# Four two-pass row tiles and six pairs, weight sums one at a time, and the pairs' products in the transposes' banks

## The chip, the cores and the metric

The kernel runs on one core of a Trainium2 chip. The metric is the device time of one execution in microseconds (us). The engines of the core work side by side, each through its own queue of instructions in order: PE (TensorE, matrix products; its weight loads are listed apart as PEld), DVE (VectorE), ACT (ScalarE), POOL (GpSimd), and SP (SyncE), which issues most of the DMAs. Products of PE go to PSUM, a memory of eight banks, and DVE or ACT take them out from there; a bank can be written again only when it has been read.

## The reference

Input x has 2048 rows of 1024 numbers (4 x 512 x 1024), all float32. Two layers follow each other, each with a residual and a layer norm:

```
attn = (w1 @ w2.T) * sparse_mask
x = layernorm(x + gelu(x @ attn + b2))
w_l, w_h = dequant(qweight, lut4, 4 bits), dequant(qweight, lut8, 8 bits)
y = where(norm(x) > 64, x @ w_h.T, x @ w_l.T) + bias
out = layernorm(x + y)
```

The mask is nonzero only in a band around the diagonal. A dequantised weight is a table entry, chosen per output row by the bits of the code, which lie in bit planes.

## The kernel before

**Tiles and stages.** The 2048 rows are 16 row tiles of 128. Weights, both as products' operands, stay in the core's memory. A first stage builds `attn` for the band and dequantises the left half of the 4-bit weight (output columns 0 to 511). The right half is dequantised in eight more steps of the generator `low` (`steps(1)`), woven into the second stage; each step is three or four predicated copies on DVE with table lines made by ACT and POOL. A finished block of the weight is transposed into `wT` by PE (`transpose_pending`), and the identity is added to the weight, so that a product already holds the residual.

**Attention tile** (`attention(n, xT)`): PE multiplies the transposed tile by the band (L467) into an accumulator `mm`, DVE adds b2 and writes `z` (L482), ACT does the gelu (L483), DVE adds x (L485), ACT sums squares (L354), POOL makes the factor (L356, L357), DVE normalises (L361).

**Two-pass tile**: `ffn_half(n, xT, h)` multiplies the transposed tile by one half of `wT` (eight matmuls 512 wide, L495, each two records in the trace), and `combine` (L507) takes the product out of `mm`. ("left", n) is h = 0, ("right", n) is h = 1; after the right one `finish_rows` normalises the row tile (the same chain of DVE, ACT, POOL and DVE) and stores it. The tile's transposed x is made once by PE, with copies out of PSUM on ACT (L263, L264), and kept under the tag `early{n}`.

**Pair** (`ffn_pair`): two row tiles are taken together as a 2 x 2 block product by the Strassen-Winograd scheme: seven products of four matmuls each instead of eight. It needs sums of weight blocks, t1 to t4 (`weight_sums`, L544 to L547, DVE), and of input blocks, s1 to s4 (`pair_inputs`: a copy of the first on ACT, s1 and s3 on DVE, a copy of a22 on ACT, s2 and s4 on POOL). Its input is transposed without PE: `squares` transposes 32 x 32 squares on DVE (L554), writes them to DRAM (L558) and reads them back in four DMAs per tile (L564, `rows`). Products go to banks u (two buffers), v and w of the pool `ps_pair`. `prepare_pair(n, part)` does one third of the preparation of the pair that starts at tile n; within a pair the next one is prepared (`between`).

**Order.** The list `todo` is the order of work of the second stage: attention of tiles 0 to 3, then lefts with attention between, two more attention tiles (8 and 9), then rights, each followed by one of the attention tiles 10 to 15. The transposes of the next entry of the list are issued ahead of the present one. At ("right", 0) all dequantisation is finished, the pool of the dequantisation is closed, the pool `last` is opened in its place, and tiles 12 to 15 of x (from `SOON` on) are loaded into it. `check_outside` reads the parts of the mask outside the band and sums their absolute values, one block at a time after a left or an attention tile. Instructions are scheduled by the program's framework in the order of the program where their dependences allow it; each engine then has a fixed list.

**PSUM.** `ps_tr` (four banks, transposes) lives to the end; `ps_mm` (two accumulators of two banks, taken in turn by attention tiles and halves) is closed before the pairs, and `ps_pair` takes its four banks. The buffer tag `z` (two buffers) is shared by z, the normalised output `o` and the mask blocks `raw`.

```
todo = [("attention", n) for n in range(4)]
for m in range(EARLY):
    todo.append(("left", m))
    if m < 4:
        todo.append(("attention", 4 + m))
todo += [("attention", 8), ("attention", 9)]
for m in range(EARLY):
    todo += [("right", m), ("attention", 10 + m)]
```

Of the kernel before, what the change touches and what calls it, by code (L numbers as in the profile page):

```python
# [9 lines left out]
FP = mybir.dt.float32  # L10
# [19 lines left out]
WIN = P + 2 * BAND  # L30
SQ = 32
Q = P // SQ
EARLY = 6
AHEAD = 2


# [156 lines left out]
def kernel(  # L193
# [13 lines left out]
    nc = tc.nc  # L207
# [6 lines left out]

    with ExitStack() as main:
        const = main.enter_context(tc.tile_pool(name="const", bufs=1))
        ps_tr = main.enter_context(tc.tile_pool(name="ps_tr", bufs=4, space=bass.MemoryType.PSUM))
        first_ps, first_sb = main.enter_context(ExitStack()), main.enter_context(ExitStack())
        ps_mm = first_ps.enter_context(
            tc.tile_pool(name="ps_mm", bufs=2, space=bass.MemoryType.PSUM)  # L220
        )
        band = main.enter_context(tc.tile_pool(name="band", bufs=1, side="right"))
        dq = first_sb.enter_context(tc.tile_pool(name="dq", bufs=1, side="right"))
# [302 lines left out]
        def ffn_half(n, xT, h):  # L526
            ps = ps_mm.tile([P, D], FP, tag="mm", name="mm")
            product(ps[:, :HALF], xT, h)
            combine(n, h, ps[:, :HALF], bias_bc[:, ts(h, HALF)])
            if h == 1:  # L530
                finish_rows(n)

# [4 lines left out]
        b11, b12 = wT[:, :KH, :HALF], wT[:, :KH, HALF:]  # L537
        b21, b22 = wT[:, KH:, :HALF], wT[:, KH:, HALF:]

        def weight_sums(pool):  # L540
            t1, t2, t3, t4 = (
                pool.tile([P, KH, HALF], FP, tag=f"t{i}", name=f"t{i}") for i in range(1, 5)
            )
            nc.vector.tensor_tensor(t1, b12, b11, ALU.subtract)  # L544
            nc.vector.tensor_tensor(t2, b22, t1, ALU.subtract)
            nc.vector.tensor_tensor(t3, b22, b12, ALU.subtract)
            nc.vector.tensor_tensor(t4, b21, t2, ALU.subtract)  # L547
            return t1, t2, t3, t4

        def squares(pool, n):  # L550

# [39 lines left out]
            nc.gpsimd.tensor_tensor(s4, a12, s2, ALU.subtract)  # L591
            return a11, a12, a22, s1, s2, s3, s4

        def ffn_pair(pool, n, blocks, weights, between):

            a11, a12, a22, s1, s2, s3, s4 = blocks
            t1, t2, t3, t4 = weights
# [35 lines left out]
        def count_odd():  # L633


            nc.vector.tensor_scalar(ssq, ssq, EST_T * EST_T, None, ALU.is_gt)
            nc.vector.tensor_scalar(outside, outside, 0.0, None, ALU.is_equal)
            nc.vector.tensor_scalar(outside, outside, -1.0, 1.0, ALU.mult, ALU.add)
            n_odd = const.tile([P, 1], FP, name="n_odd")
            nc.vector.tensor_reduce(n_odd, odd, AX.X, ALU.add)  # L640
            pc = ps_tr.tile([P, 1], FP, tag="tr", name="pc")
            nc.tensor.matmul(out=pc[0:1, :], lhsT=n_odd, rhs=ones, start=True, stop=True)
            nc.vector.tensor_copy(count, pc[0:1, :])

        todo = [("attention", n) for n in range(4)]
        for m in range(EARLY):
            todo.append(("left", m))
            if m < 4:  # L650
                todo.append(("attention", 4 + m))
        todo += [("attention", 8), ("attention", 9)]
        for m in range(EARLY):
            todo += [("right", m), ("attention", 10 + m)]
        unpack_after = [("attention", 1), ("left", 0), ("attention", 4), ("left", 1)]
        unpack_after += [("attention", 6), ("left", 2), ("left", 3), ("left", 4)]

        kept = {}
        rows, blocks = {}, {}
# [17 lines left out]
        ready = prepare(*todo[0])  # L677
        checks = 0
        for i, (what, n) in enumerate(todo):
            if (what, n) == ("right", 0):  # L680
                steps(100)
                transpose_pending(0)
                first_sb.close()
                last = main.enter_context(tc.tile_pool(name="last", bufs=1, side="right"))
                for m in range(SOON, NT):
                    load_x(last, m)
            if (what, n) == ("left", 0):
                transpose_pending(0)
            xT = ready
            if i + 1 < len(todo):  # L690
                ready = prepare(*todo[i + 1])
            if what == "attention":
                attention(n, xT)
                if n > 8 and checks < KT:
                    check_outside(checks)
                    checks += 1
            else:
                ffn_half(n, xT, 0 if what == "left" else 1)
                if what == "left" and n > 1:
                    check_outside(checks)  # L700
                    checks += 1
                if (what, n) == ("right", 0):
                    weights = weight_sums(last)
            if (what, n) in unpack_after:
                steps(1)
            if what == "right" and n >= EARLY - 3:
                prepare_pair(EARLY, n - (EARLY - 3))
        while checks < KT:
            check_outside(checks)
            checks += 1  # L710
# [4 lines left out]
        for n in range(EARLY, NT, PAIR):  # L715

            def between(part, done, m=n + PAIR):
                with tc.issue_after(done.ins):
                    prepare_pair(m, part)

            ffn_pair(ps_pair, n, blocks[n], weights, between)
            if n == EARLY:
                count_odd()

# [41 lines left out]
```

## Time and profile before

| | |
|---|---|
| median of 3 runs | 381.35 us (381.2 to 381.87) |
| the profiled execution | 380.86 us |
| its span (first to last instruction) | 379.1 us |
| first stage | 0 to 60.8 us |
| attention tiles, lefts, dequantisation | 60.8 to 172.1 us |
| rights with attention tiles | 172.1 to 245.6 us |
| five pairs | 245.6 to 368.4 us |
| last normalisation and store | 368.4 to 379.1 us |

Durations used for the change, means of one instruction from the groups: a product matmul record 0.602 us (L495; records overlap, and they follow each other every 0.43 us), squares on DVE 2.02 us (L554), a weight sum 2.29 us (L544 to L547), z 1.22 us (L482), gelu 1.05 us (L483), the add of x 1.28 us (L485), the sum of squares 1.15 us (L354), a normalisation 0.81 us (L361), a combine 0.68 us (L507). One instruction's record overlaps the next by up to 0.08 us on DVE, so that they follow each other a little faster than these.

How to read it: "the clock" is the share of TensorE's full speed that was granted. An engine's idle time is named by what ended it. A busy engine counts only where the end of the kernel hangs on it; so stages are looked at one by one.

### The profile page before, as it was taken

Reading aid. Unit: us, or ns where it says so; the run is one execution under the profiler, and the core shown is the slowest. Engines: PE = TensorE matmul, PEld = TensorE weight load, DVE = VectorE, ACT = ScalarE, POOL = GpSimd, SP = SyncE. Lnnn points to the kernel's source line nnn. Section 1 sums busy time; section 2 is a strip of 40 time slices with the busy share of each in tenths; the row PEclk is TensorE's granted clock in tenths of the full one; section 3 lists DMA queues with packets and bytes.
Section 4 is the critical chain, followed back from the end, with each engine's and each line's share of the span. In section 5 each row is a group of like instructions: output and inputs, shape, how many; then the busy total and the mean of one; then the engine's idle time right before and its main releaser. Section 6 shows DMA issues by size and latency. Waiting matters only on the chain.

```text
span 379.1 us, 3687 instructions
## 1 busy us (share of the span) xinstructions
PE 336.0 (89%) x1226; PEld 206.7 (55%) x1226; DVE 231.2 (61%) x344; ACT 149.2 (39%) x228; POOL 119.9 (32%) x144
## 2 busy tenths in 40 slices
PE   3599785989989898988999999599999999999980
PEld 3588574975666464583666656344444444444430
DVE  2599798889968895059744536453482563825221
ACT  0952843986485465244355443311111302113011
POOL 1990881866265511003022212210130400304000
PEclk9699996989999999998999999889999999999996
DMA  9998104900010111019242211107126162461102
GB/s 225 356 353 269 76 3 163 390 2 0 0 45 3 41 42 43 0 62 311 72 139 96 102 55 55 51 10 217 47 119 166 55 231 47 165 167 55 55 3 118
DMA packets 26906, 41.80 MB, mean 110 GB/s; under 512 B 7424, under 2 KB 19456, under 8 KB 26880
## 3 DMA queue, kind: packets, MB, share of 16 engines
q1 hardware_dynamic: 21616, 40.90, 31.6%
q10 hardware_dynamic: 5264, 0.59, 1.1%
q8 instruction: 11, 0.18, 0.2%
q14 instruction: 15, 0.12, 0.1%
HBM read 27.85 MB, written 13.63 MB: 109 GB/s over the span
## 4 chain that ended last, share of the span: by engine, by line
PE 42%; DVE 26%; POOL 12%; ACT 9%; issue 8%; DMA 1%; ACTq 0%; POOLq 0%; DVEq 0%
PE u L604 18%; PE w L604 9%; ACT junk L354 5%; PE mm L467 5%; PE v L604 5%; POOL root L307 4%; PE mm L495 4%; DVE root L312 3%; DVE x L485 3%; DVE root L311 3%; POOL r L357 3%; DVE z L482 3%; POOL e L307 2%; DVE e L310 2%; DVE root L316 2%
## 5 line engine op out<-in xcount | busy, mean ns | idle before, releaser
L495 PE MATMUL mm<-wT,xT 128*128 128x512 f32 x192 | 86.2, 602 | 5.4 <-DVE x L507 2.7
L356 POOL TENSOR_SCALAR r<-ss 128x1 f32<-128x1 f32 x32 | 10.4, 325 | 200.0 <-ACT junk L354 199.8
L354 ACT ACTIVATE junk<-x,nm 128x1024 bf16<-128x1024 f32 x32 | 36.8, 1149 | 82.9 <-DVE nm L351 82.7
L467 PE MATMUL mm<-attn,xT 128*128 128x198 f32 (+2 forms) x320 | 63.9, 358 | 5.3 <-ACT xT L264 5.3
L467 PEld LDWEIGHTS mm<-attn,xT 128*128 128x128 f32 x320 | 56.1, 201 | 13.7 <-ACT xT L264 5.7
L495 PEld LDWEIGHTS mm<-wT,xT 128*128 128x128 f32 x192 | 36.1, 193 | 47.2 <-issue 40.5
L303 ACT ACTIVATE e<-v,lt,diff 128x1024 f32<-128x1024 uint8 x32 | 38.2, 1240 | 11.4 <-DVE v L278 9.7
L307 POOL TENSOR_SCALAR root<-v,diff,lt 128x1024 f32<-128x1024 uint8 x16 | 36.4, 2277 | 8.2 <-DVE root L316 7.4
L307 POOL TENSOR_SCALAR e<-v,diff,lt 128x1024 f32<-128x1024 uint8 x16 | 29.6, 1852 | 28.5 <-DVE v L278 25.5
L604 PE MATMUL u<-t,halves 128*128 128x512 f32 x80 | 36.0, 592 | 0.0
L361 DVE TENSOR_SCALAR o<-x,nm,r 128x1024 f32<-128x1024 f32 x16 | 13.0, 812 | 34.4 <-POOL r L357 34.4
L421 PE MATMUL mm<-w2T,w_sb 128*128 128x268 f32 (+1 forms) x128 | 30.1, 390 | 4.1 <-issue 2.3
L264 ACT COPY xT<-pt 128x512 f32<-128x512 f32 x44 | 23.4, 583 | 23.4 <-PE pt L263 18.3
L483 ACT ACTIVATE z<-z 128x1024 f32<-128x1024 f32 x16 | 16.9, 1054 | 31.0 <-DVE z L482 31.0
L421 PEld LDWEIGHTS mm<-w2T,w_sb 128*128 128x128 f32 x128 | 24.3, 200 | 8.1 <-issue 2.5
L311 DVE COPY_PREDICATED root<-v,e 128x1024 f32<-128x1024 uint8 x16 | 22.9, 1433 | 7.8 <-POOL root L307 7.8
L310 DVE COPY_PREDICATED e<-v,e 128x1024 f32<-128x1024 uint8 x16 | 24.3, 1524 | 3.4 <-ACT e L303 3.4
L263 PE MATMUL pt<-ident,x 128*128 128x128 f32 x176 | 23.0, 275 | 3.6 <-DVE x L361 1.8
L485 DVE SCALAR_TENSOR_TENSOR x<-z,x 128x1024 f32<-128x1024 f32 x16 | 20.4, 1276 | 9.2 <-ACT z L483 9.2
L604 PEld LDWEIGHTS u<-t,halves 128*128 128x128 f32 x80 | 15.2, 190 | 19.1 <-issue 18.9
L586 ACT COPY halves<-rows 128x1024 f32<-128x1024 f32 x5 | 5.2, 1042 | 51.2 <-DMA rows<-there 39.0
L361 DVE TENSOR_SCALAR x<-x,nm,r 128x1024 f32<-128x1024 f32 x16 | 13.0, 810 | 19.3 <-POOL r L357 19.3
(74 smaller groups left out, 425.3 us busy)
## 6 DMA issues: line engine op xcount, KB each, us to landing
x<-in_L_attn_x_dram SPq DMA_DIRECT2D x16, 512.0 KB, 6.9
out_dram<-o SPq DMA_DIRECT2D x16, 512.0 KB, 2.6
there<-squares SPq DMA_DIRECT2D x10, 512.0 KB, 3.0
rows<-there SPq DMA_DIRECT2D x40, 128.0 KB, 3.4
w_raw<-in_L_attn_w_dram SPq DMA_DIRECT2D x8, 512.0 KB, 5.6
w_sb<-in_L_attn_w_dram SPq DMA_DIRECT2D x3, 1024.0 KB, 7.8
w_sb<-in_L_attn_w_dram SPq DMA_DIRECT2D x2, 512.0 KB, 5.1
raw<-_L_attn_sparse_mask_dram SPq DMA_DIRECT2D x2, 413.0 KB, 2.9
```

Source lines behind the costliest of these rows:

```text
L264: nc.scalar.copy(dst[:, g * (HALF // P) : (g + 1) * (HALF // P), :], pt)
L303: nc.scalar.activation(entry[j], plane(0), AF.Identity, scale=d_k, bias=l_k)
L307: nc.gpsimd.tensor_scalar(entry[j], plane(0), d_k, l_k, ALU.mult, ALU.add)
L310: nc.vector.copy_predicated(entry[2], plane(1), entry[3])
L311: nc.vector.copy_predicated(root, plane(1), entry[1])
L354: nc.scalar.activation(junk, u, AF.Square, bias=nm, accum_out=ss)
L361: nc.vector.tensor_scalar(dst, u, nm, r, ALU.add, ALU.mult)
L421: nc.tensor.matmul(out=ps[:, : hi - lo], lhsT=w1_sb[s][:, k, :], rhs=w2T[:, k, lo:hi], start=(k == 0), stop=(k == KT - 1),)
L467: nc.tensor.matmul(out=ps[:, a:b], lhsT=xT[:, s, :], rhs=attn[:, s, a - lo : b - lo], start=h not in fresh, stop=hi == D or (h == 0 and wi ...
L485: nc.vector.scalar_tensor_tensor(xt, z, 1.0, xt, ALU.mult, ALU.add, accum_out=total)
L495: nc.tensor.matmul(out=ps, lhsT=xT[:, k, :], rhs=wT[:, k, ts(h, HALF)], start=(k == 0), stop=(k == KT - 1),)
L604: nc.tensor.matmul(out=ps, lhsT=a[:, k, :], rhs=b[:, k, :], start=start and k == 0, stop=stop and k == KH - 1, skip_group_check=True,)
```

## The change

EARLY goes from 6 to 4: tiles 0 to 3 are two-pass tiles, tiles 4 to 15 make six pairs. The order of work follows: after the four lefts, attention tiles 8 to 11 come ahead of the rights (before: 8 and 9), and the four rights are followed by attention tiles 12 to 15. The places of the dequantisation steps in this order move up by at most one entry or two. The dequantisation is closed, `last` opened and x of tiles 12 to 15 loaded at ("attention", 10), two attention tiles ahead of the first right. The four weight sums are no longer made together at the first right: t1 is issued after the combine of right 0, t2 after that of right 1 and so on, each held back until that combine (`tc.issue_after`). The first pair's preparation comes after rights 1, 2 and 3, after the weight sum (before: after rights 3, 4 and 5). In PSUM the two pools change places: `ps_mm` lives to the end and `ps_tr` is closed before the pairs, so that the pairs' banks u, v and w are those of the transposes; the one small product of `count_odd` goes to `ps_mm`.

```
-EARLY = 6
+EARLY = 4
...
-        ps_tr = main.enter_context(tc.tile_pool(name="ps_tr", bufs=4, space=bass.MemoryType.PSUM))
+        ps_mm = main.enter_context(tc.tile_pool(name="ps_mm", bufs=2, space=bass.MemoryType.PSUM))
         first_ps, first_sb = main.enter_context(ExitStack()), main.enter_context(ExitStack())
-        ps_mm = first_ps.enter_context(
-            tc.tile_pool(name="ps_mm", bufs=2, space=bass.MemoryType.PSUM)
+        ps_tr = first_ps.enter_context(
+            tc.tile_pool(name="ps_tr", bufs=4, space=bass.MemoryType.PSUM)
         )
...
-            combine(n, h, ps[:, :HALF], bias_bc[:, ts(h, HALF)])
+            done = combine(n, h, ps[:, :HALF], bias_bc[:, ts(h, HALF)])
             if h == 1:
                 finish_rows(n)
+            return done
...
+        sums_of = {1: (b12, b11), 2: (b22, 1), 3: (b22, b12), 4: (b21, 2)}
+        weights = {}
+
+        def weight_sum(pool, i):
+
+            plus, minus = sums_of[i]
+            weights[i] = pool.tile([P, KH, HALF], FP, tag=f"t{i}", name=f"t{i}")
+            minus = weights[minus] if isinstance(minus, int) else minus
+            nc.vector.tensor_tensor(weights[i], plus, minus, ALU.subtract)
...
         for m in range(EARLY):
-            todo.append(("left", m))
-            if m < 4:
-                todo.append(("attention", 4 + m))
-        todo += [("attention", 8), ("attention", 9)]
+            todo += [("left", m), ("attention", 4 + m)]
+        todo += [("attention", n) for n in range(4 + EARLY, SOON)]
         for m in range(EARLY):
-            todo += [("right", m), ("attention", 10 + m)]
+            todo += [("right", m), ("attention", SOON + m)]
         unpack_after = [("attention", 1), ("left", 0), ("attention", 4), ("left", 1)]
-        unpack_after += [("attention", 6), ("left", 2), ("left", 3), ("left", 4)]
+        unpack_after += [("attention", 5), ("left", 2), ("attention", 6), ("left", 3)]
...
-            if (what, n) == ("right", 0):
+            if (what, n) == ("attention", SOON - 2):
                 steps(100)
                 transpose_pending(0)
                 first_sb.close()
...
-                if (what, n) == ("right", 0):
-                    weights = weight_sums(last)
+                if what == "right":
+                    with tc.issue_after(done.ins):
+                        weight_sum(last, n + 1)
+                        if n >= EARLY - 3:
+                            prepare_pair(EARLY, n - (EARLY - 3))
             if (what, n) in unpack_after:
                 steps(1)
-            if what == "right" and n >= EARLY - 3:
-                prepare_pair(EARLY, n - (EARLY - 3))
```

In the changed kernel the lines from L540 on move by one or two (the products of a pair, L604 before, are L605).

More of the change, by code (lines that the diff above doesn't have):

```diff
@@ L538 @@
         b21, b22 = wT[:, KH:, :HALF], wT[:, KH:, HALF:]
[L540 to L548, printed above, removed]
+        sums_of = {1: (b12, b11), 2: (b22, 1), 3: (b22, b12), 4: (b21, 2)}
[5 more added lines that the diff above has]
+            nc.vector.tensor_tensor(weights[i], plus, minus, ALU.subtract)
         def squares(pool, n):
@@ L592, in pair_inputs, with ffn_pair @@
             return a11, a12, a22, s1, s2, s3, s4
-        def ffn_pair(pool, n, blocks, weights, between):
+        def ffn_pair(pool, n, blocks, between):
             a11, a12, a22, s1, s2, s3, s4 = blocks
-            t1, t2, t3, t4 = weights
+            t1, t2, t3, t4 = (weights[i] for i in range(1, 5))
             u = pool.tile([P, HALF], FP, tag="u", name="u", bufs=2)
@@ L640, in count_odd @@
             nc.vector.tensor_reduce(n_odd, odd, AX.X, ALU.add)
-            pc = ps_tr.tile([P, 1], FP, tag="tr", name="pc")
-            nc.tensor.matmul(out=pc[0:1, :], lhsT=n_odd, rhs=ones, start=True, stop=True)
-            nc.vector.tensor_copy(count, pc[0:1, :])
+            pc = ps_mm.tile([P, D], FP, tag="mm", name="pc")
+            nc.tensor.matmul(out=pc[0:1, 0:1], lhsT=n_odd, rhs=ones, start=True, stop=True)
+            nc.vector.tensor_copy(count, pc[0:1, 0:1])
         todo = [("attention", n) for n in range(4)]
         for m in range(EARLY):
-            todo.append(("left", m))
-            if m < 4:
-                todo.append(("attention", 4 + m))
-        todo += [("attention", 8), ("attention", 9)]
+            todo += [("left", m), ("attention", 4 + m)]
+        todo += [("attention", n) for n in range(4 + EARLY, SOON)]
         for m in range(EARLY):
-            todo += [("right", m), ("attention", 10 + m)]
+            todo += [("right", m), ("attention", SOON + m)]
         unpack_after = [("attention", 1), ("left", 0), ("attention", 4), ("left", 1)]
-        unpack_after += [("attention", 6), ("left", 2), ("left", 3), ("left", 4)]
+        unpack_after += [("attention", 5), ("left", 2), ("attention", 6), ("left", 3)]
         kept = {}
@@ L697 @@
             else:
-                ffn_half(n, xT, 0 if what == "left" else 1)
+                done = ffn_half(n, xT, 0 if what == "left" else 1)
                 if what == "left" and n > 1:
@@ L719, in between @@
                     prepare_pair(m, part)
-            ffn_pair(ps_pair, n, blocks[n], weights, between)
+            ffn_pair(ps_pair, n, blocks[n], between)
             if n == EARLY:
```

## The prediction, made before the changed kernel had run

> **What bounds the kernel now.** I read the busy shares first, then busy time by stage, then who TensorE waited for, then the chain of work that ended last. TensorE (PE) is busy 89% of the span:
>
> ```profile
> PE 336.0 (89%) x1226; PEld 206.7 (55%) x1226; DVE 231.2 (61%) x344; ACT 149.2 (39%) x228; POOL 119.9 (32%) x144
> ```
>
> By stage (start:end, length, then busy time of PE, its weight loads, DVE, ACT, POOL, then granted clock, DMA share, GB/s): attention tiles with left halves, the last attention tiles before the right halves, right halves with attention, the five pairs.
>
> ```profile
> 60.80:163.00 102.20, 94.60 (x419) 66.79 (x420) 75.48 (x103) 61.76 (x95) 45.20 (x48) 0.96 0.18 68
> 163.00:187.00 24.00, 21.46 (x96) 14.88 (x95) 20.03 (x20) 10.49 (x19) 3.66 (x8) 0.93 0.54 175
> 187.00:245.60 58.60, 53.97 (x209) 34.06 (x207) 29.08 (x56) 26.29 (x48) 14.32 (x34) 0.98 0.20 75
> 245.60:365.20 119.60, 119.60 (x275) 52.80 (x276) 56.99 (x99) 18.41 (x27) 18.51 (x28) 0.98 0.34 109
> ```
>
> The pair stage is pure PE. In the others PE is nearly full, so its work counts one for one and its few waits count besides. The waits of PE from 60 to 260 us (waited for: total, times, longest):
>
> ```profile
> PE mm L467 <- ACT xT L264: 5.3, 2, 4.7
> PE u L604 <- DVE z L482: 4.6, 1, 4.6
> PE mm L495 <- DVE x L507: 2.7, 2, 1.4
> PE mm L495 <- ACT wT L264: 2.5, 1, 2.5
> ```
>
> The 4.6 is the first pair waiting for the last attention tile's z; the 2.5 is the first right half waiting for the last weight transposes. The chain shows why z is late (start, length, what; one right half with its attention tile):
>
> ```profile
> 205.61 0.69 DVE x L507 x2
> 206.31 0.60 DVE halves L587
> 207.28 1.25 ACT junk L354 x2
> 209.53 0.67 issue
> 210.20 1.23 DVE z L482
> 211.45 1.07 ACT z L483
> 212.54 1.24 DVE x L485 x2
> 214.07 1.25 ACT junk L354 x2
> 215.67 0.56 POOL r L357
> 216.26 0.81 DVE x L361
> 217.37 0.61 DVE x L507 x2
> ```
>
> From one combine (L507) to the next is 11.76 us, 11.1 without the 0.60 for halves. PE needs 6.87 (16 records of a half) + 3.60 (attention) + 0.87 (transposes) = 11.34 for the same iteration. So the in-order DVE queue is as long as PE's work, with about 0.2 us to spare.
>
> **What the Trainium skill says.** "TensorE: Matmul & The Clock Gate", Part 1: after an idle window of some 3.4 us PE runs at half rate for about as long. The trace agrees: after the 4.63 us wait the first eight records took 5.76 us to the next product instead of 3.43, so the wait cost 2.3 more; after 2.54 us before the first right half, 1.5 more (8.38 instead of 6.87 to the next work). The same page (Architectural detail) has ACT and DVE as strict FIFO queues, which the chain above shows. "DMA: Bandwidth & Descriptors" (Anatomy of one DMA) gives a DMA about 2 us fixed whatever its size; here squares to DRAM land in 3.0 us and rows in 3.4 (medians), so the round trip is more than two such.
>
> **The change, part by part.**
>
> (1) PE work. Tiles 4 and 5 lose two passes each (4 x 6.87) and two sets of transposes (2 x 0.87): -29.2. The sixth pair adds 7 products x 3.43 = +24.0. Net -5.2.
>
> (2) Up to the end of left half 3 (135.5 us before) nothing changes: the order of DVE is the same up to there, PE only gets one weight transpose earlier. DVE is what bounds here: z of attention 6 came at 134.26, 10 us after its products, and the last dequantisation ended at 140.5. Moving two copy-predicated instructions ahead of z delays attention 7 by nothing I can price (z at about 136.8, PE there at 137.3). The next attention tile takes the accumulator of left 3, whose combine comes behind the same dequantisation at 142.4: I keep a 1.3 us wait.
>
> (3) From 135.5 to the first right half, PE: five attention tiles 18.0, five sets of x transposes 4.35, three of weights 2.6, the wait 1.3: 26.3, so the first right half starts at 161.8 instead of 172.1. The weight transposes sit two attention tiles ahead of it, so the 2.5 wait and its slow restart of 1.5 go. Covered by: ACT copies the last wT at about 156. In return x12 to x15 are loaded after these transposes, just ahead of their use: SP issues them at about 153, the first x load of four landed 3.7 us after its issue (3.7/5.8/7.8 least, median, most), and PE reaches x12's transposes after 0.87 + 3.60 = 4.5. I take 0; if x12 came last of four, 3.3 and a restart. The mask checks are queued behind these loads on SP; their ACT instructions wait for them with the second half of x12's transposes behind, needed only 7 us later.
>
> (4) Right halves with attention 12 to 15, PE: 4 x 6.87 + 4 x 3.60 + 3 x 0.87 = 44.5. Here DVE gets new work: one weight sum of 2.2 us after each combine, a stream transpose of 1.95 after the second and third, none of which had a place in this chain before (the four sums and both transposes ran at 168 to 186, while right half 0 and one attention tile kept PE busy). The queue of the changed kernel, with the lengths of the chain above (combine 0.69, statistics 2.35 from nm to the normalisation, z 1.2, gelu 1.1, x 1.3): first iteration 13.1, second 12.1, third 12.2, against 11.34 for PE. z of attention 11 is also late, so the first combine starts 1.8 after its product. With R the end of right half 0 (168.7): combines start at R+1.8, +14.9, +27.0. Attention 14 reuses the accumulator of attention 13, whose z ends at R+24.6, where PE is ready at R+22.7: 1.9 lost. Attention 15 waits for z of 14 (R+36.8; ready at R+36.0): 0.8. Bounds: nothing, if the two accumulators absorb it; 6, if each stop also restarts slowly. I take 2.7 and 0.5 for one partial restart.
>
> (5) Start of the pairs. Their four banks are now those of the transposes, free once ACT has copied the last xT, long before: the 4.6 wait and the 2.3 restart go. Late next is s1 of tiles 4 and 5: the stream transpose of tile 5 ends at R+34.7, DRAM and back 3.2 + 1.7 of issues + 3.0 gives rows at R+42.6, s1 at R+43.3 to 44; PE wants it one product after its start, at R+43.9. Behind that waiting instruction on DVE stand the last normalisation, s3, the first add of the pair, z and x of attention 15 and two more stream transposes, on POOL s2; on SP the rows are behind one store, on ACT the copy of a22 holds gelu of 15. Adds must free u and w within 6.87 us: the second is 0.4 late. I take 0.6; between 0 and 4.
>
> (6) Pairs: six of 24.03 = 144.2, +0.3 as the five showed (122.8 = 120.2 + 2.3 + 0.3). After the last product 10.7 us as before (368.4 to 379.1).
>
> Sum: 161.8 + 44.5 + 3.2 + 0.6 + 144.5 + 10.7 = 365.3 us of span, 13.8 less. The profiled execution took 380.86 for a span of 379.1, that is 1.8 around it: 367.1. The median of the runs, 381.35, is 0.5 higher than the profiled one, half of which I add: 367.3.
>
> **The rivals.**
>
> A: DVE keeps up and neither stop happens: 3.8 less, 363.5. For it: durations on DVE overlap by some 0.08 us each, and two accumulators allow a lag of several us. Against it: the chain of before left only 0.2 us and it gets 2.2 to 4.2 more per iteration.
>
> B: the x loads come late. All four share 16 DMA engines, and a mask check before them in SP's queue waits for a buffer. PE then idles 3.3 before attention 11 and restarts slowly (2.3): 367.3 + 5.6 = 372.9. For it: in the trace these loads and the squares kept the DMA engines over 90% busy for 10 us. Against: no squares go out at that time now, and x12 is first in the queue.
>
> C, slower than before: the added DVE work, with rows arriving late, stops PE in each right-half iteration long enough to halve the clock. One such stop costs its idle plus 2.3 us; to lose the 14 us gained it takes four of 3.5 + 2.3 = 23.2 in place of my 3.8, so 367.3 + 19.4 = 386.7. It decides once an iteration of the queue passes about 11.34 + 3.6 = 15 us (4 x 3.6 = 14.4 more). For it: written with nothing overlapped, an iteration of that queue is 15.4. Against: the new order puts combine and nm of the next tile between the waits, which brings it to 12.2.
>
> Not a rival with its own time but part of (2): if dequantisation is late, removed left halves only turn into waits; that costs up to 3.
>
> **How the numbers follow.** Forecast 0.60, A 0.18, B 0.15, C 0.04, anything else 0.03 (two thirds of it faster). The range takes in A with 1 us of margin and B: 362.5 to 372.9. 0.2% (0.8 us) is what a measurement can tell from no change: faster 0.95, same 0.01, slower 0.04.
>
> **What would show it.** Right: no wait of the first u product for z; first right half near 162 with no wait for wT; 6 x 24 us of pairs; short waits of the attention products (L467) for z in the right-half stage, 2 to 4 us in all. Wrong: a DMA wait at the transposes of x12 (B); PE below full clock between 170 and 210, or the w product waiting for halves (C); PE full in that stage (A).

## The result, and the profile after

The changed kernel takes 376.09 us (median of 4 runs, 375.64 to 376.31) against 381.61 us for the kernel before beside it (4 runs, 381.2 to 382.13): a ratio of 0.9853, 95% interval 0.9836 to 0.987. It is faster, by 5.5 us instead of the 14 forecast, and lies 3.2 us above the top of the range.

The profiled execution took 375.64 us for a span of 373.9. The page's busy times and shares of the span:

```profile
PE 327.9 (88%) x1202; PEld 199.9 (53%) x1202; DVE 238.4 (64%) x351; ACT 147.9 (40%) x226; POOL 125.0 (33%) x146
```

PE is busy 8.1 us less than before (the work taken away is 5.2, and two products that ran slowly after waits are gone besides), and the span is only 5.2 shorter: waits have come in. The stages of the changed kernel, in the columns of the table of stages before (attention tiles ahead of the rights, rights with attention, first pair and the door of the second, the other pairs):

```profile
135.60:164.50 28.90, 26.06 (x166) 23.35 (x165) 18.98 (x28) 18.96 (x36) 5.91 (x16) 1.00 0.28 100
164.50:212.20 47.70, 44.95 (x170) 27.74 (x169) 30.33 (x46) 22.25 (x44) 8.12 (x22) 1.00 0.34 110
212.20:242.00 29.80, 26.16 (x62) 10.70 (x61) 19.12 (x31) 8.36 (x14) 7.89 (x14) 1.00 0.31 90
242.00:362.00 120.00, 119.10 (x278) 52.54 (x277) 58.26 (x103) 18.62 (x28) 21.05 (x29) 1.00 0.36 114
```

PE idles 2.8 us in each of the first two and 3.6 in the third, and 0.9 in the last, where the pairs of before, once begun, had no idle time at all. The granted clock is 1.00 in all of them, so none of this is a slow restart. PE's waits of the changed kernel from 60 to 260 us (total, times, longest):

```profile
PE mm L467 <- ACT xT L264: 5.7, 3, 4.7
PE pt L263 <- ACT wT L264: 3.6, 3, 1.7
PE u L605 <- DVE x L618: 2.9, 2, 2.0
PE mm L467 <- DVE z L482: 2.8, 2, 1.9
...
PE w L605 <- DVE nm L351: 1.2, 1, 1.2
PE w L605 <- DVE halves L588: 0.4, 1, 0.4
```

The wait of the first u product for z (4.6) is gone, and so is that of the first right half for wT (2.5). New are the waits for z (L482) in the rights' stage, and those of products u and w in the first two pairs for additions on DVE (L618, and L620 behind the small nm L351) and for s1 (L588). The chain of work of one right half with its attention tile, in the changed kernel (start, length, what):

```profile
185.82 0.61 DVE x L507 x2
186.43 2.21 DVE t L549
...
188.71 1.94 DVE squares L555
...
190.80 1.25 ACT junk L354 x2
...
192.40 0.56 POOL r L357
...
193.71 1.23 DVE z L482
194.96 1.07 ACT z L483
196.05 1.25 DVE x L485 x2
```

Between combine and z stand now a weight sum and a stream transpose, 4.15 us of work that was not there before. The combines start at 172.76, 185.74, 197.39 and 210.73, 12.7 apart in the mean; PE needs 11.34 for each iteration. PE had finished right 3 at 206.65, so DVE comes to the pairs 4.1 us behind. In the kernel before it was 2.9 (right 5 ended at 237.37, its combine began at 240.22), so not all of this is new. What DVE does at the door of the pairs is seen in the timelines of the changed kernel's first pair. First PE (start, length, operation; in brackets the idle time before and what ended it):

```profile
212.21 3.60 PE L605 MATMUL u<-wT,halves 128*128 128x512 f32 x8
216.24 3.70 PE L605 MATMUL w<-t,halves 128*128 128x512 f32 x8 [0.44 <-DVE halves L588]
221.94 3.67 PE L605 MATMUL u<-t,halves 128*128 128x512 f32 x8 [2.00 <-DVE x L618]
226.81 3.67 PE L605 MATMUL w<-wT,halves 128*128 128x512 f32 x8 [1.20 <-DVE nm L351]
```

The third product is added onto the first in the bank u, so it waits until the addition L618 has read the first out; the fourth waits in the same way for the addition on w (L620). DVE in the same stretch:

```profile
210.73 0.69 DVE L507 SCALAR_TENSOR_TENSOR x<-mm,bias_bc 128x512 f32<-128x512 f32 x1
...
211.41 2.28 DVE L549 TENSOR_TENSOR t<-wT,t 128x2048 f32<-128x2048 f32 x1
...
215.50 0.69 DVE L588 TENSOR_TENSOR halves<-rows 128x512 f32<-128x512 f32 x1
217.78 1.75 DVE L361 TENSOR_SCALAR o<-x,nm,r 128x1024 f32<-128x1024 f32 x1 [1.59 <-POOL r L357]
219.45 1.74 DVE L589 TENSOR_TENSOR halves<-rows 128x512 f32<-128x512 f32 x1
221.12 0.68 DVE L618 TENSOR_TENSOR x<-u,bias_bc 128x512 f32<-128x512 f32 x1
```

And POOL:

```profile
217.71 1.27 POOL L591 TENSOR_TENSOR halves<-halves 128x512 f32<-128x512 f32 x1
219.05 1.59 POOL L592 TENSOR_TENSOR halves<-halves 128x512 f32<-128x512 f32 x1
```

The addition (L618) could have run at 215.8, when its product was done, but stands behind o, which waits for right 3's statistics, and behind s3. Both took a microsecond longer than the 0.81 and 0.69 us that they take elsewhere, exactly while POOL made s2 and s4.

### The profile page after: what moved, and what is told of

It is laid out like the page before. It is cut to its first block, busy times and chain, and to the rows that moved or that the text cites. A ratio compares the mean times of both kernels' runs of the same rounds, so it can differ in the third digit from the quotient of the medians.

```text
span 373.9 us, 3676 instructions
## 1 busy us (share of the span) xinstructions
PE 327.9 (88%) x1202; PEld 199.9 (53%) x1202; DVE 238.4 (64%) x351; ACT 147.9 (40%) x226; POOL 125.0 (33%) x146
## 4 chain that ended last, share of the span: by engine, by line
PE 35%; DVE 25%; POOL 17%; ACT 12%; issue 8%; DMA 1%; ACTq 0%; POOLq 0%; DVEq 0%
PE u L605 18%; PE w L605 9%; POOL root L307 7%; PE v L605 6%; ACT junk L354 5%; POOL e L307 4%; DVE x L485 4%; DVE root L312 3%; POOL r L357 3%; DVE z L482 2%; DVE root L316 2%; ACT z L483 2%; PE mm L467 2%; DVE t L549 2%; DVE e L310 2%
## 5 line engine op out<-in xcount | busy, mean ns | idle before, releaser
L467 PE MATMUL mm<-attn,xT 128*128 128x198 f32 (+2 forms) x320 | 62.9, 353 | 8.5 <-ACT xT L264 5.7
L467 PEld LDWEIGHTS mm<-attn,xT 128*128 128x128 f32 x320 | 54.4, 196 | 16.9 <-ACT xT L264 6.5
L495 PE MATMUL mm<-wT,xT 128*128 128x512 f32 x128 | 56.5, 594 | 1.6 <-DVE x L507 1.6
L605 PE MATMUL u<-t,halves 128*128 128x512 f32 x96 | 43.4, 595 | 2.9 <-DVE x L618 2.9
L307 POOL TENSOR_SCALAR root<-v,diff,lt 128x1024 f32<-128x1024 uint8 x16 | 38.9, 2433 | 8.1 <-DVE root L316 7.4
L495 PEld LDWEIGHTS mm<-wT,xT 128*128 128x128 f32 x128 | 23.7, 190 | 28.9 <-issue 26.3
L605 PEld LDWEIGHTS u<-t,halves 128*128 128x128 f32 x96 | 18.0, 190 | 26.8 <-issue 25.8
L587 ACT COPY halves<-rows 128x1024 f32<-128x1024 f32 x6 | 6.3, 1047 | 58.4 <-DMA rows<-there 46.5
L311 DVE COPY_PREDICATED root<-v,e 128x1024 f32<-128x1024 uint8 x16 | 22.7, 1416 | 8.8 <-POOL root L307 8.8
L264 ACT COPY xT<-pt 128x512 f32<-128x512 f32 x40 | 21.4, 587 | 10.2 <-DVE attn L428 5.1
L312 DVE COPY_PREDICATED root<-v,e 128x1024 f32<-128x1024 uint8 x16 | 24.7, 1547 | 0.1
```

The source lines that it names most:

```text
L307: nc.gpsimd.tensor_scalar(entry[j], plane(0), d_k, l_k, ALU.mult, ALU.add)
L311: nc.vector.copy_predicated(root, plane(1), entry[1])
L312: nc.vector.copy_predicated(root, plane(2), entry[2])
L467: nc.tensor.matmul(out=ps[:, a:b], lhsT=xT[:, s, :], rhs=attn[:, s, a - lo : b - lo], start=h not in fresh, stop=hi == D or (h == 0 and wi ...
L495: nc.tensor.matmul(out=ps, lhsT=xT[:, k, :], rhs=wT[:, k, ts(h, HALF)], start=(k == 0), stop=(k == KT - 1),)
L605: nc.tensor.matmul(out=ps, lhsT=a[:, k, :], rhs=b[:, k, :], start=start and k == 0, stop=stop and k == KH - 1, skip_group_check=True,)
```

## The experiments

The question is where 8.6 us of the forecast went: the span is 373.9 and not 365.3. The theory: DVE's in-order queue, which carries the sums and the transposes of the first pair through the rights' stage, arrives late at the pairs, and hands its lateness to PE as waits for the additions. Rivals: the rows of the first pair come late by DMA; the earlier dequantisation steps cost the time before right 0; the buffers of z are held by the mask checks; the banks alone did it all.

Each kernel was timed beside the kernel before; times are medians, ratios are to the kernel before with their 95% intervals.

**The kernel before with the two pools exchanged, and nothing else.** EARLY stays 6.

```
-        ps_tr = main.enter_context(tc.tile_pool(name="ps_tr", bufs=4, ...))
+        ps_mm = main.enter_context(tc.tile_pool(name="ps_mm", bufs=2, ...))
...
-        ps_mm = first_ps.enter_context(tc.tile_pool(name="ps_mm", bufs=2, ...))
+        ps_tr = first_ps.enter_context(tc.tile_pool(name="ps_tr", bufs=4, ...))
```

> The kernel before with nothing but the banks swapped (six two-pass tiles, five pairs, sums together). The wait of 4.6 us for z and the slow restart of 2.3 go, and no new wait comes, since s1 and s3 are ready early there: theory 1 and my reckoning of the banks: 374 to 376. Rival (the first adds of the pair then wait behind the last attention tile's work on DVE, as in the changed kernel): 377 to 380.

376.03 us, ratio 0.9866 (0.985 to 0.9883): as fast as the whole change, within the intervals. The first product u starts at 240.18 instead of 245.60. PE's waits in the pairs of this kernel:

```profile
PE u L604 <- DVE nm L351: 1.7, 1, 1.7
PE w L604 <- DVE x L619: 0.6, 1, 0.6
```

The 4.6 us wait for z and its restart are gone, and 2.3 us of waits for additions have come, the same kind as in the changed kernel but smaller; s1 and s3 do not stand ahead of the first addition here. Of the 5.1 us by which this execution's span is shorter than before, 4.2 are at the pairs (the wait and the first pair took 4.63 + 26.57 us before, the first pair 27.01 here). Another 1.4 are not the edit's: after the same 2.54 us wait for wT, right half 0 took 8.54 us before and 7.13 here. About 0.5 is lost again elsewhere.

**The changed kernel with the products of the pairs in the old banks.** The opposite: the pools go back, all else is as in the changed kernel.

> The changed kernel with the pairs' products in the two accumulators' banks, as before the change. z of the last attention tile ends at 222.9 in the changed kernel, 10.7 after PE reaches the first pair. Theory 1 (DVE is behind there): PE waits 7 to 10 us for that z and restarts slowly, while the 3.6 us of waits inside the first pair shrink; time 379 to 383. Rival (the banks are not what counts, since DVE must finish the same work either way): 376 to 377.5.

383.53 us, ratio 1.0065 (1.0043 to 1.0088): slower than before. The first product of the pairs on PE in this kernel:

```profile
222.47 5.26 PE L605 MATMUL u<-wT,halves 128*128 128x512 f32 x8 [10.00 <-DVE z L482]
```

Ten microseconds, where the kernel before waited 4.6: z of attention 15 comes 10 us after PE has reached the pairs, and the old banks wait for all of it. The first pair itself is then short (25.9 us), because DVE has caught up meanwhile. So without the banks, the four two-pass tiles and six pairs are worth less than nothing, and with them nothing that can be told from the noise: 376.03 and 376.09.

**The steps of dequantisation at later places.**

```
-        unpack_after += [("attention", 5), ("left", 2), ("attention", 6), ("left", 3)]
+        unpack_after += [("left", 2), ("attention", 6), ("left", 3), ("attention", 7)]
```

> The changed kernel with the last four dequantisation steps one entry later again (after left 2, attention 6, left 3, attention 7, instead of attention 5, left 2, attention 6, left 3). Theory 1 (earlier steps put predicated copies ahead of the add of x of attention 6 on DVE, so that ACT's copies of wT, queued behind the sum of squares, free the transposes' banks late): the waits of PE's transposes for ACT wT between 135 and 165 us fall from 1.9 to under 0.5, right half 0 starts at 162 to 163 instead of 164.5, time 374 to 375 against 376.1. Rival (the chain of attention on DVE sets the pace there whatever the order): right half 0 within 0.5 us of 164.5 and the time within 0.5 of 376.1.

375.98 us, ratio 0.9861 (0.9845 to 0.9878). Right half 0 starts at 164.78 and not earlier (164.47 in the changed kernel); the waits for ACT's copies only stand at other products. The first pair takes the same waits to the hundredth (0.44, 2.00, 1.20). Moving these four steps by one entry changes nothing in the end.

**One weight sum for four.** t2, t3 and t4 are left out and t1 stands for them, which takes three sums of 2.3 us off DVE.

```
+            if i > 1:
+                weights[i] = weights[1]
+                return
```

> The changed kernel with t1 used in place of t2, t3 and t4, so three of the four weight sums are left out (6.6 us of DVE work after rights 1, 2 and 3). Theory 1 (DVE's queue from right 0 to the first pair's adds is what is late): the two waits of the attention products for z (0.9 and 1.9) go, the first pair starts at about 209.4 instead of 212.2 and takes 24 to 25.5 us instead of 28.9; time 368.5 to 371. Rival 1 (the rows' way through DRAM is late): the pair's start gains 2.8, but the first pair still takes 27 or more; 373. Rival 2 (s2 and s4 on POOL hold up DVE's normalisation and s3 beside them): the wait of the third product for its first add stays near 2; 371 to 372.

373.7 us (371.47 to 375.23), ratio 0.9782 (0.9745 to 0.9818): only 2.4 us for 6.9 us less work on DVE. But the profiled execution is the slowest of the four, and two products ran slowly in it: an attention product ahead of right half 0 took 5.51 us where it took 3.83 in the changed kernel, and the w product below 6.64 instead of 3.70. Without these two it would be some 4.6 us shorter, by an estimate from these figures, so 2.4 may be too low for what the sums cost. In the rights' stage most of the excess goes (45.27 us instead of 47.74; the least is 44.5), but the w product of the first pair now waits longer for s1. PE in this kernel:

```profile
211.41 3.60 PE L608 MATMUL u<-wT,halves 128*128 128x512 f32 x8
217.92 6.64 PE L608 MATMUL w<-t,halves 128*128 128x512 f32 x8 [2.91 <-DVE halves L591]
```

and DVE:

```profile
213.08 0.68 DVE L507 SCALAR_TENSOR_TENSOR x<-mm,bias_bc 128x512 f32<-128x512 f32 x1
...
216.45 0.81 DVE L361 TENSOR_SCALAR o<-x,nm,r 128x1024 f32<-128x1024 f32 x1 [2.30 <-POOL r L357]
217.18 0.69 DVE L591 TENSOR_TENSOR halves<-rows 128x512 f32<-128x512 f32 x1
```

Counted from the start of right half 0 (166.14 here, 164.47 in the changed kernel) the last combine is no earlier, 46.9 us instead of 46.3, though two of the three sums stood ahead of it: the scheduler put the attention tile's normalisation ahead of the combine, and the queue holds an idle wait of 2.3 us for each row's statistics (DVE to ACT to POOL and back), twice per iteration. s1 stood behind such a wait (o), ready to run without it: DVE took it directly behind o, with no DMA named, 51.0 us after the start of right half 0 in both kernels. The first addition came 1.9 us earlier. So the queue's length is waits as much as work, and work that is taken out of it where it had filled a wait is not gained in full. That s1 was ready also speaks against the rows coming late.

**The mask checks two attention tiles earlier**, so that their blocks don't hold a buffer of z in the rights' stage.

```
-                if n > 8 and checks < KT:
+                if n > 6 and checks < KT:
```

> The changed kernel with the mask checks two attention tiles earlier (from attention 7 on instead of 9), so that none stands between attention 13 and the first pair. The z of attention 14 waited 1.18 us for ACT's check (its buffer is shared with the mask blocks), and PE 1.9 for that z. Theory 1 (DVE's queue is what is late; the shared buffer is one link of it): the 1.18 goes, the first pair starts about 1 us earlier, time 374.5 to 375.5. Rival (the buffers shared with the checks are the main cause of the late z): both waits for z (0.9, 1.9) go and the first pair loses most of its 3.6 us, 370 to 372.

375.83 us, ratio 0.9847 (0.9813 to 0.988). The waits for z fall from 2.76 to 1.6 us, and the first pair has waits of 2.08 for s1 and 3.12 for the first addition in their place. The buffer is a link in the chain, not its cause.

**The last right's normalisation behind the first addition.** `finish_rows(3)` is issued after the first addition of the first pair, so that o no longer stands ahead of it.

```
-            if h == 1:
+            if h == 1 and n < EARLY - 1:
                 finish_rows(n)
...
                 with tc.issue_after(done.ins):
+                    if m == EARLY + PAIR and part == 0:
+                        finish_rows(EARLY - 1)
                     prepare_pair(m, part)
```

> The changed kernel with the normalisation and store of tile 3 issued after the first add of the first pair instead of after right 3. In the changed kernel that normalisation (which waits for POOL) and s3 stand ahead of the first add of the pair on DVE, each 0.9 to 1.0 us longer than alone because s2 and s4 run on POOL beside them. Theory 1: the first add comes 2 to 3 us earlier, the 2.0 wait of the third product falls under 0.7, the first pair takes 25.5 to 27 us; time 372.5 to 374. Rival (the queue is only put in another order, and the late adds wait for the same sum of work): the 2.0 turns into a longer wait of the fourth or fifth product, time 375 to 377.

378.41 us, ratio 0.9916 (0.9885 to 0.9946), slower than the changed kernel. The first pair gets shorter (27.28 us instead of 28.88), but its preparation of the next pair is pushed back, and s1 and the additions of pairs 2 to 4 are late in turn (25.1, 25.6 and 25.5 us instead of 25.27 and twice 24.03). Lateness on DVE that is put off is paid in the next pairs.

**The weight sums in the waits for statistics.** t1 to t3 are issued between the statistics and the normalisation of attention tiles 10 to 12, t4 after right 0.

```
             nm, r, ss = stats(xt, total)
+            gap()
             normalize(xt, xt, nm, r)
...
-                attention(n, xT)
+                attention(n, xT, lambda: 9 < n <= SOON and weight_sum(last, n - 9))
```

> The changed kernel with the weight sums t1 to t3 issued within attention tiles 10 to 12 (the scheduler puts them between the add and the normalisation, where DVE waited 1 to 2.6 us) and t4 after right 0, so that none follows rights 1 to 3. Theory 1 (the sums in DVE's queue of the right-half stage are what makes the first pair late, and they fit in the waits before it): both waits of the attention products for z go, the first pair starts at 209 to 210.5 and takes 25 to 27.5; time 369.5 to 372. Rival (no slack on DVE there either): right half 0 or 1 starts later by what is gained after, 375 to 377.

374.74 us, ratio 0.9838 (0.9803 to 0.9874), not told apart from the changed kernel. The pairs start 1.5 us earlier (210.68), and the w product then waits 3.05 us for s1, behind o on DVE as in the run with one sum, and runs slowly after it (5.40 us).

**The stream transposes out of the rights' stage.** The squares of tiles 4 and 5 are transposed after attention 10 and 11, and the first pair's inputs are made after right 2 instead of right 3.

```
                 attention(n, xT)
+                if n in (SOON - 2, SOON - 1):
+                    prepare_pair(EARLY, n - (SOON - 2))
...
-                        if n >= EARLY - 3:
-                            prepare_pair(EARLY, n - (EARLY - 3))
+                        if n == EARLY - 2:
+                            prepare_pair(EARLY, PAIR)
```

> The changed kernel with the stream transposes of tiles 4 and 5 at attention 10 and 11 and the rest of the first pair's inputs after right 2, so that only the sums are new in the right-half stage and s1 to s4 are made 11 us ahead of the first pair. Theory 1: the iterations of DVE's queue fall to about 11 to 13, the waits for z shrink to under 1.5 in all, and the first pair's waits to under 1.5: 370.5 to 372.5. Rival 1 (rows late): now excluded, as rows land 20 us ahead; if the first pair still waits 3 us or more for its adds, it is the queue alone: 373 to 375. Rival 2 (the transposes delay attention 10 and 11): right half 0 starts 2 to 4 later and the time stays at 375 or more.

370.03 us (369.53 to 371.16), ratio 0.9712 (0.9679 to 0.9745): 6 us better than the changed kernel. Its rights' stage takes 45.93 us, its first pair 26.41, its second 24.14, and right half 0 starts 0.8 earlier: 1.8 + 2.5 + 1.1 + 0.8 = 6.2 us, the whole of the difference in span (367.7). PE's waits in the pairs of this kernel:

```profile
PE u L605 <- DVE x L618: 1.3, 1, 1.3
PE mm L467 <- DVE z L482: 1.2, 1, 1.2
PE w L605 <- DVE x L620: 0.2, 1, 0.2
```

**The same transposes early, the inputs after right 3 as in the change.** Only the first half of the edit above.

> As the run with the stream transposes at attention 10 and 11 (370.0), but the first pair's sums and copies of inputs stay after right 3, as in the changed kernel. Tells the transposes in the right-half queue from the inputs at the pair's door. Theory 1a (the transposes in the queue are what costs): the pair starts at 209 to 210.5 as there, and time is 370 to 371.5. Theory 1b (s1 to s4 just ahead of the pair's adds, with POOL beside DVE): the first pair's waits come back to 3 us or more, 372 to 374.

371.61 us (370.45 to 372.68), ratio 0.9749 (0.9717 to 0.978). The rights' stage is at its minimum (44.48 us, no wait for z left), and the first pair takes 28.97, its third product:

```profile
218.64 5.37 PE L605 MATMUL u<-t,halves 128*128 128x512 f32 x8 [2.79 <-DVE x L618]
```

So the two halves of the edit act in two places: the transposes decide the rights' stage, the place of s1 to s4 the first pair. The second half adds little on top, though: in time the two kernels are not told apart, of the 2.6 us by which this first pair is longer than with both halves (26.41), 1.7 are the slow product shown, and the rights' stage is 1.45 shorter (44.48 against 45.93).

The two runs also tell what the lateness itself does. Here the last combine was 1.4 us behind the end of its product (206.76 and 205.39), with both halves 3.5 (208.26 and 204.72); still the first addition came later here, 8.99 us after the start of the pair against 7.50. What stands ahead of the addition on DVE counted for more than the lateness brought along.

**Transposes early, and the sums spread out**: t1 in attention 11, t2 and t3 after rights 0 and 1, t4 in the first pair.

```
             nm, r, ss = stats(xt, total)
+            if n == SOON - 1:
+                weight_sum(last, 1)
...
-                        weight_sum(last, n + 1)
+                        if n < 2:
+                            weight_sum(last, n + 2)
```

> As the run with the stream transposes early (370.0), with the weight sums spread besides: t1 within attention 11, t2 and t3 after rights 0 and 1, t4 within the first pair after its fourth product. Theory 1: what is left of waits there (1.2 for z of attention 14, 1.3 and 0.2 for the first pair's adds) goes: 367 to 369. Rival (what is left is the chain of statistics alone, without the sums): 369.5 to 370.5.

372.7 us (5 runs, 372.46 to 373.32), ratio 0.9774 (0.9754 to 0.9794): worse than leaving the sums after the combines. The rights' stage is as short as it can be (44.5), but the first pair waits 3.06 us for its first addition, which came to stand behind o, z and x of attention 15. That is not what makes the profiled execution long: of the 3.8 us by which its span exceeds that of the early transposes, 3.4 lie before right half 0 (167.05 instead of 163.68), and 3.05 of them are one attention product, earlier than anything that the edit moves, which took 3.83 us there:

```profile
145.18 6.88 PE L467 MATMUL mm<-attn,xT 128*128 128x198 f32 x20 [0.84 <-ACT xT L264]
```

From the start of right half 0 to the end of the second pair the two kernels differ by 0.5 us (96.99 and 96.48). The trace doesn't show that spreading the sums costs more than that, and what made the other four executions longer is not seen.

**s2 and s4 of the first pair on DVE**, in the changed kernel: is it POOL that stretches o and s3?

```
+            eng = nc.vector if n == EARLY else nc.gpsimd
-            nc.gpsimd.tensor_tensor(s2, s1, a11, ALU.subtract)
-            nc.gpsimd.tensor_tensor(s4, a12, s2, ALU.subtract)
+            eng.tensor_tensor(s2, s1, a11, ALU.subtract)
+            eng.tensor_tensor(s4, a12, s2, ALU.subtract)
```

> The changed kernel with s2 and s4 of the first pair alone on DVE instead of POOL. If it is POOL's two additions beside them that stretch DVE's normalisation o (1.75 us) and s3 (1.74 us), o falls to about 0.81 and s3 to about 0.69, s2 and s4 take about 0.7 each, the first add y11 starts within 0.7 us of where it did (221.1; 2 x 0.7 more in the queue, 2.0 less of stretching), z of attention 15, which now stands between s2 and s4, starts some 2 us earlier (about 219.8), and the time stays within 1 us of 376.1. Rival: the two are long because of their own operands (rows just landed, squares read across), then o and s3 stay at 1.7 and the first add comes 1.4 us later with the first pair 1 to 2 us longer.

374.23 us (373.21 to 374.8), ratio 0.9813 (0.979 to 0.9836). DVE in this kernel (s2 is L592, the first addition L619):

```profile
218.16 0.81 DVE L361 TENSOR_SCALAR o<-x,nm,r 128x1024 f32<-128x1024 f32 x1 [1.59 <-POOL r L357]
218.88 0.68 DVE L589 TENSOR_TENSOR halves<-rows 128x512 f32<-128x512 f32 x1
219.48 0.69 DVE L592 TENSOR_TENSOR halves<-halves 128x512 f32<-128x512 f32 x1
220.09 1.22 DVE L482 TENSOR_TENSOR z<-mm,b_bc 128x1024 f32<-128x1024 f32 x1
```

o and s3 are back at 0.81 and 0.68: the stretching was POOL's. The first addition comes no earlier for it (9.24 us after the pair's start instead of 8.91), as the two subtractions and z of attention 15 now stand ahead of it; the second does, and its wait of 1.20 is gone, so that the pair takes 27.77 us instead of 28.88. The second pair lost its wait of 0.90 as well (24.13 us), which had not been expected: the order on POOL has changed there, with the factor r of the statistics ahead of s2 and s4 instead of behind them. Together 2.2 us; the span is 1.9 shorter, as right half 0 started 0.3 later.

**Both: transposes early, inputs after right 2, and s2 and s4 of the first pair on DVE.**

> The kernel with the stream transposes of tiles 4 and 5 in attention 10 and 11 and the pair's inputs after right 2, with s2 and s4 of the first pair on DVE as well. There POOL's two additions (1.66 and 1.27 us, beside right 3) delayed the normalisation behind them on POOL, not DVE's s1 and s3 (0.69 and 0.68 us). If contention between the two engines counts, the last combine comes about 0.5 us earlier and the time falls by 0 to 1 us from 370.0; if DVE's queue is simply full, 1.4 us more of work on it make the first pair start or run about 1 us later (371).

369.39 us (368.68 to 370.31), ratio 0.968 (0.9663 to 0.9696), the lowest median of all, though not told apart from the 370.03 without the last edit. The rights' stage has no wait for z left (44.57 us instead of 45.93); the first pair is the same (26.40). In the profiled execution right half 0 started 2.1 us later, which hid this gain; the last section shows why.

## Why the prediction was off

Its sum, term by term, against the profile of the changed kernel:

| step | predicted | measured | difference |
|---|---|---|---|
| (3) start of right half 0 | 161.8 | 164.47 | +2.7 |
| (4) rights' stage | 44.5 + 3.2 | 47.74 | 0.0 |
| (5) and the first pair | 24.03 + 0.6 | 28.88 | +4.25 |
| (6) second pair, and the 0.3 | 24.33 | 25.27 | +0.9 |
| (6) four more pairs | 96.1 | 96.1 | 0.0 |
| (6) tail | 10.7 | 11.4 | +0.7 |
| span | 365.3 | 373.9 | +8.6 |

**(1) held**: the pairs after the second take 24.03 us each as before, and the two-pass tiles' work has gone.

**(3) was 2.7 too early.** The 2.5 us wait for wT did go and the x loads were in time: the first transpose of x12 ran at 159.57 us without a wait. But the only wait that I kept was 1.3 us, where the trace has four of 1.67, 0.84, 0.16 and 0.17 us for ACT's copies of wT and xT. In the trace these copies stand on ACT behind the sum of squares of attention 6, whose addition of x came at 139.33 us where it came at 136.65 before, because on DVE the predicated copies of an earlier step stand ahead of it, which step (2) had taken to delay nothing. The waits are 1.5 us more in all. Another 1.0 went where each stop breaks the overlap of PE's instructions: a set of transposes lasts 1.14 from a standing start, where sets in a row follow each other every 0.87. Moving the last four steps one entry later did not bring right half 0 forward, so their place alone is not the cause; what else keeps it near 164.5 was not settled.

**(4) was right in its mechanism, and its sum in part by luck.** Two waits for z of 0.90 and 1.86 us make 2.76 against 2.7, and 0.5 came for what surrounds them. But they were forecast the other way round, 1.9 for attention 14 and 0.8 for attention 15. The larger one holds something that the step left out: z of attention 14 waited 1.18 us for its buffer, which a mask check held.

```profile
195.07 3.83 PE L467 MATMUL mm<-attn,xT 128*128 128x198 f32 x20 [0.90 <-DVE z L482]
207.23 1.23 DVE L482 TENSOR_TENSOR z<-mm,b_bc 128x1024 f32<-128x1024 f32 x1 [1.18 <-ACT raw L455]
208.51 3.86 PE L467 MATMUL mm<-attn,xT 128*128 128x198 f32 x20 [1.86 <-DVE z L482]
```

With the checks earlier that wait was 0.72. Without this link the step would have stood about a microsecond too high. That the transposes and sums make them was shown by the runs: with one sum or with early transposes they shrink or vanish.

**(5) is the step that failed.** That the 4.6 us wait and its restart would go was right, and shown from both sides by the two runs on the banks. But what was to be late next was mis-sized, 0.6 us with an upper bound of 4 for what became 4.85. Three waits of 0.44, 2.00 and 1.20 are 3.64 of it; 1.0 is the broken overlap at these stops, and 0.2 the small product of `count_odd` (0.19, it ends the first pair; the forecast had it in the 0.3 of step (6)). Step (5) let s1 wait for rows from DRAM, and reckoned the additions as if they only had to follow the products by less than 6.87 us. In the trace the rows are not the last thing: their last DMA was issued at 208.9 and had landed by 213.0 at the latest, and s1 ran at 215.50, in its turn on DVE. What was missing is the list of what DVE has ahead of the first addition: a weight sum, two exposed statistics waits (0.72 and 1.59), s1, o and s3. So the addition began 8.91 us after the start of the pair, where the third product wants its result after 6.87. The lateness of the queue comes on top, 4.1 us at the door against 2.9 in the kernel before. I carried the queue into the accumulators (4) and not into u and w (5). The run with the inputs late, where the lateness was 1.4 and the addition still came after 8.99, speaks for the list as the larger part.

A second part is that I took o and s3 at the 0.81 and 0.69 us of rows in which POOL did nothing beside them. "SBUF — State Buffer", section "SBUF: two separate sides", of the Trainium skill says that VectorE and GpSimd share one pair of ports, and that a VectorE instruction in a two-port mode or with two inputs in SBUF, or a GpSimd instruction, holds the pair for its whole length if it starts first, while the other stands still. The trace agrees in the main: o began 0.07 us after s2 and ended 0.55 after it, s3, which has two inputs in SBUF, began during s4 and ended 0.55 after it. That o, with one such input, runs in a two-port mode is not shown here. The two were stretched by 2.0 us together; the run with s2 and s4 on DVE, which pays for these two on DVE instead, still took 1.1 us off the first pair.

**(6) missed the second pair's wait** of 0.90: r of the first pair's second tile is queued on POOL behind s2 and s4 of the second pair, and the addition behind o that waits for it. The tail's 0.7 is the last store, 6.2 us from the end of o to the end of the span instead of 5.5; why stays open.

**What it comes to.** The forecast of 14 us was about 7 for the banks and 7 for four two-pass tiles and six pairs. The first is real but smaller, 4.2 us at the pairs in the run with the banks alone, net of the new waits that it uncovers. The second was given back whole: 5.2 us of PE work and the wT wait went, and waits for ACT's copies (3), for z (4) and for the additions on DVE (5) took their place. Transposes and inputs made early win 6 to 7 us of the same waits, which makes a kernel of 369.4 to 370.0 us, shorter than either.

Of the rivals, A and B can be ruled out by the trace (waits for z are there; x loads cause none). Of C one sign came, the w product waiting for s1 (0.44), but PE stopped in only two of the four iterations, for 0.90 and 1.86 us, and its clock stayed at 1.00: far from the size at which C decides. With the old banks it is a ten-microsecond stop at one place that makes the kernel slower.

## What to carry to other kernels

When an in-order engine is found to be longer than the bottleneck's iteration, list what it still has ahead of the first thing that the next stage waits for, idle waits included, and put the lateness that it brings along on top: neither ends at the stage's border. Count a queue's length with its idle waits, and take work out where the queue has work, not where it fills a wait. Compare executions stage by stage, for one slow product in a place that the edit doesn't touch can be 1.7 to 3 us. A wait for a bank that is removed is worth what remains after the next wait behind it, so look what the same engine has to do directly after.

## What the runs showed of the hardware

**POOL is held up by DVE too, and not only the reverse.** In the kernel with early transposes an instruction for the factor of the statistics on POOL, 0.19 us at its shortest, took 1.41 beside a weight sum that ran on DVE from 208.86 to 211.15:

```profile
209.79 1.41 POOL L356 TENSOR_SCALAR r<-ss 128x1 f32<-128x1 f32 x1 [5.97 <-ACT junk L354]
211.28 0.55 POOL L357 TENSOR_TENSOR r<-r,minus_half 128x1 f32<-128x1 f32 x1
```

It ended at 211.20, 0.05 us after the sum. So a one-column instruction in the chain of the normalisation lasted until a weight sum of 2.29 us had ended. In the changed kernel the same happened at 212.91 (0.82 us).

**The slow restart of PE is no fixed price.** After waits of about the same length the next product took quite different times: 3.67 us after 2.00 (the changed kernel), 3.67 after 3.12 (checks early), 3.67 after 3.06 (sums spread), but 5.37 after 2.79 (transposes early, inputs late), 6.64 after 2.91 (one sum) and 5.40 after 3.05 (sums in the waits). It even came after two short ones, in the kernel with early transposes and s2 and s4 on DVE:

```profile
143.29 1.14 PE L263 MATMUL pt<-ident,x 128*128 128x128 f32 x8 [1.67 <-ACT wT L264]
145.28 5.51 PE L467 MATMUL mm<-attn,xT 128*128 128x198 f32 x20 [0.84 <-ACT xT L264]
```

The same attention product with the same two waits before it took 3.83 us in the changed kernel. Ten of the profiled executions have these two waits, alike to 0.03 us: in six the product took 3.83, in three 5.51 and in one 6.88 (the sums spread). Here the difference is 1.7 of the 2.1 us by which right half 0 came later in that execution. "TensorE: Matmul & The Clock Gate", Part 1, of the Trainium skill gives an idle window of some 3.4 us; here single waits of 2.8 to 2.9 us were enough and 3.12 was not. The prediction took the 2.54 us before the first right half as agreeing with it, but that wait is shorter than the window, and after the same 2.54 us the kernel with only the banks exchanged did not run slowly (7.13 us instead of 8.54). What decides between them these runs don't show.
